# Summing attention weights on TensorE in place of VectorE, and moving small routing steps to GpSimd, in a kernel of two attentions and two expert layers

## The chip, the cores and the metric

The kernel runs on one core of a Trainium2 chip. The metric is the time of one execution on the device in microseconds (us), as the median of several runs. A core has five engines that run their own instruction streams in order and wait for one another by semaphores: TensorE (PE in the profile; its weight loads are listed as PEld), VectorE (DVE), ScalarE (ACT), GpSimd (POOL) and SyncE (SP), which issues most transfers. GpSimd issues the transfers that gather or scatter rows by a list of indices. All values here are 32-bit floats, save for some small bfloat16 tiles that are named below.

## The reference

Two layers, each an attention over a context and a feed-forward layer of eight experts, of which each row uses two. `x` is 4 x 512 x 256, the context 4 x 1601 x 256. The change lies in the second layer.

```python
x = x + _L0_xattn_ref(ctx_1024, _layernorm(x, axis=-1), ...)
x = x + _L0_ffn_ref(_layernorm(x, axis=-1), ...)
x = x + _L1_xattn_ref(ctx_1024, _layernorm(x, axis=-1), L1_xattn_Wq, L1_xattn_Wk, L1_xattn_Wv, 1, 0, 1)
x = x + _L1_ffn_ref(_layernorm(x, axis=-1), L1_ffn_W1, ...)
...
# _L1_xattn_ref: 8 heads of 32
attn = jnp.einsum('bhnd,bhmd->bhnm', q, k) * scale
attn = jax.nn.softmax(attn, axis=-1)
x = jnp.einsum('bhnm,bhmd->bhnd', attn, v)
...
# _L1_ffn_ref: the two largest logits of a row weigh its experts
logits = xf @ Wr + br
topv, _ = lax.top_k(logits, TOPK)
masked = jnp.where(logits >= topv[:, TOPK - 1:TOPK], logits, -jnp.inf)
weights = jax.nn.softmax(masked, axis=-1)
```

## The kernel before

The kernel runs in four stages: the first attention (up to about 1582 us of the span), the first expert layer (to 1885), the second attention (to 2430) and the second expert layer. The change touches the third, with one small piece at the end of the second.

**Units and passes.** The second attention is cut into 16 units: 4 batches, 2 groups of 4 heads, 2 halves of 256 queries. The 1601 keys are 13 tiles of 128 (the last has 65), taken in pairs, so a unit has 7 key pairs, 0 to 6; pair 6 is a single tile. `PER_UNIT` is 7. One loop (L1763) makes a pass for each pair of each unit. A pass does, in this order:

- `weights` (L1530): for the pair of this pass, PE writes four PSUM banks, one for each head. First it adds the negated row maxima (L1538, from the bfloat16 tile `below`), then the scores (L1548, keys by queries). ScalarE takes the exponentials into two tiles `pT` of 128 x 1024 (L1562); for pair 0 these tiles are named `sum`.
- `weigh` (L1573, matmul L1581): PE multiplies the weights of the pair of the pass before (`held`) with the values, into the left half of the PSUM tile `ps_o`.
- `add_weights` (L1568): if the held pair is in `ADDED`, VectorE adds its two tiles onto the `sum` tiles of the unit (L1571).
- `maxima` (L1264): PE computes a part of the scores of the next unit the other way round, queries by keys (L1281), into four more banks, and VectorE reduces each bank to row maxima (L1292). There are seven such parts a unit, the last of them short. They run ahead of the unit that uses them: those of unit u from pass 4 of unit u-2 to pass 3 of unit u-1, where the short one falls.
- `total` (L1590, matmul L1600): the sums of weights that the softmax divides by. PE multiplies weight tiles with ones, into the right half of `ps_o`. It does so for a held pair that is neither 0 nor in `ADDED`, and, when pair 6 is held, for the `sum` tiles too.
- `closing` (L1609), when pair 6 was held: the tile is copied out, turned back by PE two passes later (L1619, L1620), divided by the sums on VectorE (L1628, L1630) and added to `x` on GpSimd (L1637).
- a list of side work, `at[step]`.

So with `ADDED = (1, 3, 5)` VectorE adds in passes 2, 4 and 6 of a unit, and PE sums in passes 3 and 5 (pairs 2 and 4) and in pass 0 of the next unit (pair 6 and the `sum` tiles).

**PSUM.** Seven banks, handed out in turn, serve the weights, the maxima and all side work. A pass takes eight without side work, so the fourth bank of a pass's weights is the one that the first bank of the maxima before it held.

**Maxima to row.** `negated` (L1299) of unit u is put at the end of pass 4 of unit u-1: VectorE reduces the parts to `most` (L1303), then splits it into three bfloat16 pieces in the tile `shift`: three casts (L1311) and two subtractions (L1313), each on 128 x 8. `to_row` (L1315), at the end of pass 5, turns `shift` by a matmul (L1317), and ScalarE writes `below` from it (L1319), which L1538 of the next unit reads. `negated` of unit 0 runs in the stage before.

**Side work.** `project(b)` computes keys and values of batches 2 and 3 (L1166, L1182). `queries(b)` normalises `x` of the next batch (statistics on VectorE, the rows `xn` on GpSimd, L181), turns it (L194) and projects it (L1241). `collect` and `add_collected` gather rows of the first expert layer and add them to `x`, both on GpSimd (L359, L360, L379, L380). `route2(b)` routes batch b for the second expert layer, in some 28 parts spread over passes by the tuples `routed` and `last_routed`: normalised rows `pay` on GpSimd (L455, L463), logits, the two choices `hot`, the weights `wb`, a count of the rows that each expert has so far (`cnt`, `earlier`, `taken2`), from which PE computes places (L543, L546), and 16 scatters by GpSimd (L591). `by` in it is GpSimd for batches 0 to 2; for batch 3, which runs in the last stage, it is VectorE.

**Order.** The whole loop stands inside `in_order(*computing)` (L1753): PE, VectorE, ScalarE and GpSimd each execute in the order in which the program was written. An instruction that waits holds up all that is behind it on its engine.

```python
of = [(s, pTs)] if s and s not in ADDED else []
if s == PER_UNIT - 1:
    of.append((0, sums.pop(u)))
...
for u in range(1, n_units):
    put(PER_UNIT * (u - 1) + 4, lambda u=u: negated(u))
    put(PER_UNIT * (u - 1) + 5, lambda u=u: to_row(u))
```

Of the kernel before, what the change touches and what calls it, by code (L numbers as in the profile page):

```python
# [12 lines left out]
ALU = mybir.AluOpType  # L13
# [5 lines left out]
B, S, D = 4, 512, 256  # L19
# [28 lines left out]
FEW = (1, 5)  # L48
NOWHERE = 65536.0
PER_UNIT = -(-NM // 2)  # L50
ADDED = (1, 3, 5)

# [28 lines left out]
def xattn_ffn_twice(ctx: ExitStack, tc: tile.TileContext, a: dict, out: bass.AP):  # L83
    nc = tc.nc
# [315 lines left out]
    taken2 = const.tile([P, E], F32, name="taken2")  # L400
    nc.vector.memset(taken2, 0.0)
    taken_a = const.tile([P, E], F32, name="taken_a")
# [4 lines left out]
    extra = const.tile([P, NX, E], F32, name="extra")  # L407
# [29 lines left out]
    def route2(b, two, psum, tag, first=0, n=NT):  # L437

        by = nc.vector if b == B - 1 else nc.gpsimd
# [13 lines left out]
        pay = two.tile([P, n, PAY], F32, tag="pay", name="pay")  # L453
# [31 lines left out]
        def wide(name):  # L485
            return two.tile([P, n, E], F32, tag=name, name=name)
# [4 lines left out]
        def spread(t):  # L491
            return t.unsqueeze(2).to_broadcast([P, n, E])


        lg, wb, keep, rest = wide("lg"), wide("wb"), wide("keep"), wide("rest")
# [11 lines left out]
        nc.vector.tensor_reduce(tot, wb, AX.X, ALU.add)  # L507
        nc.vector.reciprocal(tot, tot)
        nc.vector.tensor_tensor(wb, wb, spread(tot), ALU.mult)
        nc.vector.tensor_copy(pay[:, :, D + 1 :], wb)  # L510
        yield


# [1 line left out]
        hot, chosen = [], []  # L515
# [10 lines left out]
                yield  # L526
        mine_b = slice(b * NT + first, b * NT + first + n)
        nc.vector.tensor_reduce(over[:, mine_b], rest, AX.X, ALU.add)
        nc.vector.tensor_tensor(extra[:, mine_b, :], rest, wb, ALU.mult)
        yield  # L530


        cnt, earlier = wide("cnt2"), wide("earlier2")
        nc.vector.tensor_tensor(cnt, hot[0], hot[1], ALU.add)
        for t in range(n):
            nc.vector.tensor_copy(earlier[:, t, :], taken2)
            nc.vector.tensor_tensor(taken2, taken2, cnt[:, t, :], ALU.add)
        if b == B - 2:
            nc.vector.tensor_copy(taken_a, taken2)
        yield  # L540
        ps = psum.tile([P, n, E], F32, tag=tag, name="ps_c2")
        flat = "p t e -> p (t e)"
# [61 lines left out]
        for t0 in range(0, n, 2):  # L604
            ps = psum.tile([P, 2, D], F32, tag=tag, name="ps_b2")
            for k in range(2):
                t = t0 + k
# [62 lines left out]
    with ExitStack() as st:  # L670
# [379 lines left out]
        for n in range(n_steps + 4):  # L1050
            b, h, t = n // (H0 * NT), n // NT % H0, n % NT
# [203 lines left out]
    rest = M // 512 * 512  # L1255
# [43 lines left out]
    def negated(u):  # L1299

        most = turns.tile([P, HG, 2], F32, tag="most", name="most")
        left = turns.tile([P, HG, 2], F32, tag="left", name="left")
        nc.vector.tensor_reduce(  # L1303
            most, tops[u].rearrange("q t i n -> q i t n"), AX.X, ALU.max, negate=True
        )
        tops.pop(u)
        part = shift[u % 2].rearrange("q (i c) -> q i c", i=HG)
        for k in range(PARTS):
            to = part[:, :, 2 * k : 2 * k + 2]
            of = left if k else most  # L1310
            nc.vector.tensor_copy(to, of)  # L1311
            if k + 1 < PARTS:
                nc.vector.tensor_tensor(left, of, to, ALU.subtract)  # L1313

    def to_row(u):  # L1315
        ps = banks["m"].tile([P, P], F32, tag="m", name="ps_r")
# [12 lines left out]
    with ExitStack() as st:  # L1329
# [117 lines left out]
        def keys_next():  # L1447
            *kv, steps = keys_values(ps_s, "s", 1)
            kvs.append(kv)
            steps[6:6] = [lambda: add_collected(0, got0)]  # L1450
            steps = iter(steps)
            asking = queries(0, qTs)

            for few, asks in ((4, 0), (5, 0), (3, 1), (0, 1), (2, 1), (0, 1), (1, 1), (1, 1), (0, 1)):
                for _ in range(few):
                    next(steps)()
                for _ in range(asks):
                    next(asking)
                yield
            assert next(steps, None) is None  # L1460

            firsts = [(0, g) for g in range(len(pieces))] + [(1, g) for g in range(3)]
            for k, (u, g) in enumerate(firsts):
                maxima(u, g)
                if (u, g) == (0, len(pieces) - 1):
                    negated(0)
                yield
                if k == 0:
                    next(asking)
                    assert next(asking, None) is None  # L1470
                if (u, g) == (1, 0):
                    to_row(0)
                if k % 2 == 0:
                    yield
# [34 lines left out]
    with ExitStack() as st:  # L1509
# [58 lines left out]
        def add_weights(u, s, pTs):  # L1568
            if s in ADDED:
                for to, pT in zip(sums[u], pTs):  # L1570
                    nc.vector.tensor_tensor(to, to, pT, ALU.add)  # L1571
# [18 lines left out]
        def total(u, s, pTs, ps):  # L1590

            of = [(s, pTs)] if s and s not in ADDED else []
            if s == PER_UNIT - 1:
# [105 lines left out]
# [4 lines that stand above are left out]
# [25 lines left out]
        for b in range(B):  # L1728
            s0 = per_batch * b
            if b:  # L1730
                place(s0, route2(b - 1, one, side, "s"), routed if b + 1 < B else last_routed)
            if b + 1 < B:
                got, steps = collect(b + 1)
                first = s0 if b == 0 else s0 - 14
                for k, f in enumerate(steps):
                    put(first + (k // 2 if b == 0 else k), f)
                for t in range(NT):
                    put(
                        (first + 4 if b == 0 else first + 7) + t // 2,
                        lambda b=b, got=got, t=t: add_collected(b + 1, got, (t,), nc.gpsimd),  # L1740
                    )
                place(s0, queries(b + 1, qTs), asked[b + 1])
# [45 lines left out]
    with ExitStack() as st:  # L1788
# [246 lines left out]
        def routing():  # L2035
            yield from route2(B - 1, two, ps_t, "t")
            yield from table()

        rest = routing()
# [14 lines left out]
        for i in range(n):  # L2054
            w, xT, to, share = here
# [153 lines left out]
```

## Time and profile before

| what | us |
|---|---|
| median of 3 runs | 2731.01 |
| lowest and highest of them | 2725.08, 2732.44 |
| the profiled execution | 2725.71 |
| its span, first to last instruction | 2724.0 |
| second attention in it | 1884.8 to 2430.0 |

The profile is one execution, recorded by the hardware. In its views a row names the line of the kernel, the engine and the operation, the tile that is written and those that are read, and how often. "Idle before" is time in which the engine had nothing to run, with what ended it. Matmuls overlap, so durations of single matmuls are not to be added; from the start of one group to the start of the next is the time that counts. A product of 32-bit values shows as two matmul instructions. A product whose output has 32 rows or whose contraction is 32 long uses a quarter of the array, and four of them for the four heads run side by side.

| second attention: line | what | count |
|---|---|---|
| L1548 PE | scores for the weights | 1664 |
| L1581 PE | weights by values | 1664 |
| L1281 PE | scores for the maxima | 936 |
| L1600 PE | sums by ones | 896 |
| L1292 DVE | row maxima | 408 |
| L1571 DVE | adds onto `sum` | 96 |

The counts are of instructions, of all forms and input tiles of a line.

### The profile page before, as it was taken

The page shows a single profiled execution, that of the slowest core. Times are in us where ns is not written, and L with a number is a line of the kernel's source. Part 1 is how long each engine was busy: PE and PEld are TensorE (multiplying, and loading weights), DVE is VectorE, ACT ScalarE, POOL GpSimd, SP SyncE. Part 2 cuts the span into 40 slices and gives each one's busy share as a digit, 9 for nine tenths or more (in the row PEclk, how much of TensorE's full clock was granted, in tenths as well). Part 3 has the DMA queues.
Part 4 walks back from the last instruction along what each step waited for, and adds up shares of the span by engine and source line. Part 5 has one row for each costly group of instructions (what it writes and reads, how often), then busy time and mean ns, then how long its engine had stood idle before and what let it go on. Part 6 is the DMA issues. An engine that isn't in the chain of part 4 may idle for free. (4 is left out here: it accounts for less than half of the span.)

```text
span 2724.0 us, 38199 instructions
## 1 busy us (share of the span) xinstructions
PE 2644.8 (97%) x14620; PEld 1795.0 (66%) x14620; DVE 1363.8 (50%) x2461; ACT 919.9 (34%) x1577; POOL 352.2 (13%) x372
## 2 busy tenths in 40 slices
PE   6999999999999999999999999899999999999998
PEld 3666676676666666767666678776454454468887
DVE  6444547544466544455444441124777878753111
ACT  4322334332334332333233221122444444452221
POOL 0000000100000100000100001102432421222542
PEclk9999999999999999999999999999999999999999
DMA  5444434433443343343343455453433200025673
GB/s 178 111 115 116 99 94 111 107 90 94 104 112 88 103 99 92 90 99 91 101 104 96 122 175 174 162 168 107 126 115 106 73 19 8 19 87 190 190 230 81
DMA packets 191323, 302.89 MB, mean 111 GB/s; under 512 B 41783, under 2 KB 113272, under 8 KB 188440
## 3 DMA queue, kind: packets, MB, share of 16 engines
q1 hardware_dynamic: 152392, 218.33, 28.8%
q0 software_dynamic: 14160, 46.31, 5.8%
q10 hardware_dynamic: 24576, 35.68, 5.2%
q8 instruction: 118, 1.93, 0.3%
q14 instruction: 77, 0.63, 0.1%
HBM read 111.46 MB, written 51.07 MB: 60 GB/s over the span
## 5 line engine op out<-in xcount | busy, mean ns | idle before, releaser
L949 DVE TENSOR_REDUCE top<-ps_s 128x1 f32<-128x2113 f32 x128 | 301.8, 2358 | 584.9 <-PE ps_s L941 584.0
L978 PE MATMUL ps_o<-pT,v 128*128 128x256 f32 x2176 | 519.5, 380 | 0.0
L941 PE MATMUL ps_s<-kT,qT 128*128 128x512 f32 (+1 forms) x1280 | 489.2, 526 | 6.1 <-ACT attn L955 5.9
L978 PEld LDWEIGHTS ps_o<-pT,v 128*128 128x128 f32 x2176 | 408.1, 190 | 110.7 <-issue 65.4
L955 ACT ACTIVATE attn<-ps_s,top 128x2113 f32<-128x2113 f32 x128 | 259.2, 2025 | 477.4 <-DVE top L949 458.4
L941 PEld LDWEIGHTS ps_s<-kT,qT 128*128 128x128 f32 x1280 | 241.7, 190 | 252.4 <-issue 236.0
L970 DVE STREAM_TRANSPOSE pT<-swapped 128x2176 f32<-128x2176 f32 x128 | 312.4, 2441 | 31.4 <-DMA swapped<-attn 22.5
L1292 DVE TENSOR_REDUCE tops<-ps_s 128x1 f32<-128x512 f32 (+2 forms) x428 | 251.5, 650 | 126.3 <-PE ps_s L1281 119.0
L887 PE MATMUL ps_k<-kvin,wkv 128*128 128x512 f32 (+2 forms) x640 | 259.3, 528 | 2.9 <-DVE kvin L807 2.4
L924 PE MATMUL ps_v<-wkv,kvin 128*128 128x256 f32 x1088 | 255.3, 381 | 2.2 <-ACT v L931 1.6
L1562 ACT ACTIVATE pT<-ps_w 128x512 f32<-128x512 f32 (+1 forms) x384 | 184.8, 567 | 140.4 <-PE ps_w L1548 138.4
L924 PEld LDWEIGHTS ps_v<-wkv,kvin 128*128 128x128 f32 x1088 | 204.7, 190 | 38.6 <-issue 6.0
L903 ACT ACTIVATE kT<-ps_k,bqk 128x512 f32<-128x512 f32 (+1 forms) x192 | 101.2, 556 | 260.4 <-PE ps_k L887 125.9
L887 PEld LDWEIGHTS ps_k<-kvin,wkv 128*128 128x128 f32 x640 | 115.7, 191 | 74.8 <-issue 63.3
L931 ACT COPY v<-ps_v 128x512 f32<-128x512 f32 x144 | 80.3, 562 | 212.9 <-PE ps_v L924 131.2
L1281 PE MATMUL ps_s<-kv,qT 32*128 32x512 f32 (+1 forms) x1024 | 129.1, 557 | 2.6 <-DVE got L1630 2.5
L1548 PE MATMUL ps_w<-qT,kv 32*128 32x256 f32 (+1 forms) x1664 | 120.4, 387 | 0.0
L1571 DVE TENSOR_TENSOR sum<-sum,pT 128x1024 f32<-128x1024 f32 x96 | 114.9, 1239 | 6.3 <-ACT pT L1562 6.3
L654 PE MATMUL ps_h<-sxT,w 128*128 128x256 f32 (+1 forms) x512 | 109.6, 371 | 4.0 <-DVE sxT L644 2.5
L1345 PE MATMUL ps_y<-w,hT 128*128 128x256 f32 x480 | 108.7, 382 | 0.0
L741 POOL TENSOR_TENSOR x<-x,bo 128x256 f32<-128x256 f32 x16 | 11.7, 762 | 742.2 <-DVE lat L181 544.9
L654 PEld LDWEIGHTS ps_h<-sxT,w 128*128 128x128 f32 x512 | 92.7, 192 | 21.5 <-issue 4.2
(317 smaller groups left out, 2766.9 us busy)
## 6 DMA issues: line engine op xcount, KB each, us to landing
swapped<-attn SPq DMA_DIRECT2D x1536, 68.0 KB
swapped<-attn ACTq DMA_DIRECT2D x512, 68.0 KB
w<-in_w_dram SPq DMA_DIRECT2D x32, 1024.0 KB
rows_b<-empty SPq DMA_DIRECT2D x36, 530.0 KB
w_e<-in_wall_dram SPq DMA_DIRECT2D x5, 2052.0 KB
cw<-in_ctxT_dram SPq DMA_DIRECT2D x4, 1601.0 KB
ctx_b<-in_ctx_dram SPq DMA_DIRECT2D x3, 1536.0 KB
slot_x<-scrap SPq DMA_DIRECT2D x8, 512.0 KB
```

The lines of the kernel that those rows point to most:

```text
L654: nc.tensor.matmul(ps[:, f, :], lhsT=w1[:, c, (f0 + f) * P : (f0 + f + 1) * P], rhs=sxT[:, c, :], start=c == 0, stop=c == DC - 1,)
L887: nc.tensor.matmul(ps[:, :n], lhsT=wkv[:, c, hs], rhs=kvin[:, c, : n // 32, k, :] if k < 4 else flat_kvin[c][:, left : left + P], start=c ...
L924: nc.tensor.matmul(ps[:, k, :], lhsT=flat_kvin[c][:, j * P : (j + 1) * P], rhs=wkv[:, c, cols], start=c == 0, stop=c == DC - 1,)
L941: nc.tensor.matmul(flat[:, j0 : j0 + n], lhsT=qT[:, t * P : (t + 1) * P], rhs=kT[:, j0 : j0 + n], start=True, stop=True,)
L949: nc.vector.tensor_reduce(top, flat[:, :L], AX.X, ALU.max, negate=True)
L955: nc.scalar.activation(attn[:, :L], flat[:, :L], AF.Exp, bias=top, accum_out=total)
L970: nc.vector.transpose(pT[:, :, k * P : (k + 1) * P].rearrange("p c (a i) -> p a c i", a=4), swapped.rearrange("p a (c i) -> p a c i", i=32),)
L978: nc.tensor.matmul(ps, lhsT=v[:, j - parts[part][0], (h % 2) * DH0 : (h % 2 + 1) * DH0], rhs=pT[:, j, :], start=j == 0, stop=j == NB - 1,)
L1281: nc.tensor.matmul(pss[i][:, at : at + n], lhsT=qTs[b][rows, o, q0 : q0 + P], rhs=kvs[b][0][o][rows, j0 : j0 + n], start=True, stop=True,)
L1292: nc.vector.tensor_reduce(tops[u][:, t : t + at // n, some, j0 // 512], of, AX.X, ALU.max,)
L1548: nc.tensor.matmul(pss[i][:r, k * QH : (k + 1) * QH], lhsT=kvs[b][0][o][rows, j * P : j * P + r], rhs=qTs[b][rows, o, f * QH : (f + 1) * Q ...
L1562: nc.scalar.activation(pT[:r, i, :n], pss[2 * h + i][:r, :n], AF.Exp)
```

## The change

`ADDED` becomes `(3,)`: VectorE adds only pair 3, in pass 4. Pairs 1 and 5 take the road of pairs 2 and 4: in passes 2 and 6 `total` multiplies their tiles with ones on PE. In `route2` a copy of the weights into `pay`, the product `extra` and the whole carried count go by `by`, which is GpSimd for batches 0 to 2. In `negated` the casts and subtractions go to GpSimd; the reduction to `most` stays on VectorE.

```diff
-ADDED = (1, 3, 5)
+ADDED = (3,)
...
-        nc.vector.tensor_copy(pay[:, :, D + 1 :], wb)
+        by.tensor_copy(pay[:, :, D + 1 :], wb)
...
-        nc.vector.tensor_tensor(extra[:, mine_b, :], rest, wb, ALU.mult)
+        by.tensor_tensor(extra[:, mine_b, :], rest, wb, ALU.mult)
...
         cnt, earlier = wide("cnt2"), wide("earlier2")
-        nc.vector.tensor_tensor(cnt, hot[0], hot[1], ALU.add)
+        by.tensor_tensor(cnt, hot[0], hot[1], ALU.add)
         for t in range(n):
-            nc.vector.tensor_copy(earlier[:, t, :], taken2)
-            nc.vector.tensor_tensor(taken2, taken2, cnt[:, t, :], ALU.add)
+            by.tensor_copy(earlier[:, t, :], taken2)
+            by.tensor_tensor(taken2, taken2, cnt[:, t, :], ALU.add)
         if b == B - 2:
-            nc.vector.tensor_copy(taken_a, taken2)
+            by.tensor_copy(taken_a, taken2)
...
         for k in range(PARTS):
             to = part[:, :, 2 * k : 2 * k + 2]
             of = left if k else most
-            nc.vector.tensor_copy(to, of)
+            nc.gpsimd.tensor_copy(to, of)
             if k + 1 < PARTS:
-                nc.vector.tensor_tensor(left, of, to, ALU.subtract)
+                nc.gpsimd.tensor_tensor(left, of, to, ALU.subtract)
```

## The prediction

> **What bounds the kernel now.** I read the page's busy table and slices first, then the stage of the change (the second attention, 1884.8 to 2430.0 us of the span) by windows, then PE's own timeline there, and last the lists of groups and waits.
>
> ```profile
> PE 2644.8 (97%) x14620; PEld 1795.0 (66%) x14620; DVE 1363.8 (50%) x2461; ACT 919.9 (34%) x1577; POOL 352.2 (13%) x372
> ...
> 1884.80:2430.00 545.20, 521.17 (x6050) 265.34 (x6053) 415.55 (x923) 262.00 (x553) 174.75 (x190) 0.98 0.22 67
> 1884.80:2160.00 275.20, 266.54 (x3059) 133.86 (x3062) 215.81 (x472) 134.70 (x286) 102.02 (x118) 1.00 0.34 102
> 2160.00:2310.00 150.00, 142.89 (x1652) 72.41 (x1648) 115.50 (x261) 70.82 (x148) 38.09 (x38) 0.99 0.10 36
> 2310.00:2402.00 92.00, 84.51 (x940) 43.26 (x940) 70.44 (x168) 38.41 (x82) 20.50 (x21) 0.89 0.05 15
> ```
>
> The columns of the windows are length, then busy time of PE, PEld, DVE, ACT and POOL, granted clock, DMA share, GB/s. PE is busy 521 of 545 us and DVE 416. So PE sets the pace, DVE has 130 us to spare, and VectorE work that is taken away is worth only the time that PE waits for it. The reader should also see the last row: 0.89 of the clock.
>
> PE's timeline gives those waits. The loop makes seven passes a unit; pass s runs L1538 and L1548 for key pair s, and L1581, the maxima L1281 and the sums L1600 for the pair before. Passes 6 and 0 of one unit:
>
> ```profile
> 2266.90 0.53 PE L1538 MATMUL ps_w<-below,ones_b 6*65 6x256 bf16 x4
> 2267.17 0.69 PE L1548 MATMUL ps_w<-qT,kv 32*65 32x256 f32 x8
> 2267.80 1.07 PE L1581 MATMUL ps_o<-pT,kv 128*32 128x256 f32 x16
> 2268.80 1.14 PE L1281 MATMUL ps_s<-kv,qT 32*128 32x512 f32 x8
> 2269.76 0.39 PE L1538 MATMUL ps_w<-below,ones_b 6*128 6x512 bf16 x3
> 2271.23 0.37 PE L1538 MATMUL ps_w<-below,ones_b 6*128 6x512 bf16 x1 [1.08 <-DVE tops L1292]
> ...
> 2274.56 1.05 PE L1600 MATMUL ps_o<-sum,ones 128*32 128x256 f32 x16
> ```
>
> ```profile
> 2268.23 2.35 DVE L1571 TENSOR_TENSOR sum<-sum,pT 128x1024 f32<-128x1024 f32 x2
> 2270.49 2.48 DVE L1292 TENSOR_REDUCE tops<-ps_s 128x1 f32<-128x512 f32 x4
> ```
>
> The fourth L1538 takes the bank of the first maxima; that reduction stands on DVE behind the two adds of key pair 5. Maxima started on PE at 2268.80, their reduction at 2270.49, PE went on at 2271.23. A start-to-start length shows the whole loss: L1538 takes 0.23 us where nothing waits and 1.48 here, and L1548 behind it 1.16 in place of 0.96.
>
> **The change, part by part.** *Sums on PE.* Pairs 1 and 5 leave VectorE in 16 units: 2 x 2 x 16 = 64 of the 96 adds, 64 x 1.24 = 79 us of DVE, nothing on the path by themselves. PE gains 2 pairs x 2 tiles x 4 heads = 16 products a unit, each two instructions in the trace, 512 in all. Sixteen L1600 take 1.00 us start to start in the passes that have them now (3, 5), so 32 x 1.00 = 32.0 us more PE time, all on the path; ends 0.95 and 1.05 a pass, 30.4 and 33.6.
>
> ```profile
> L1571 DVE TENSOR_TENSOR sum<-sum,pT 128x1024 f32<-128x1024 f32 x96 | 114.9, 1239 | 6.3 <-ACT pT L1562 6.3
> ...
> L1600 PE MATMUL ps_o<-pT,ones 128*32 128x256 f32 (+1 forms) x640 | 46.3, 400 | 0.0
> ```
>
> *Waits that go.* Adds of pairs 1 and 5 sit in passes 2 and 6, so the waits behind them are at the starts of passes 3 and 0. I took the length of each such pass from the first L1538 to the next pass's, less its side work, against the shortest of its kind: 3.80 us for pass 3 (units 5 and 9), 4.43 for pass 0 (unit 9). Half-clock stretches of L1581 and L1600 are left out here. Pass 3, units 0 to 14: 1.5, 1.5, 0.7, 1.5, 0.7, 0, 1.5, 2.2, 0.5, 0, 1.6, 1.3, 1.5, 2.6, 3.9, together 21.0. Pass 0, units 1 to 14: 0.6, 0.2, 0.6, 0.2, 0.1, 1.4, 0.5, 0.2, 0.2, 0.2, 1.5, 1.6, 0.7, 1.4, together 9.4. Maxima held up inside pass 6 of three units: 3 x 0.4 = 1.2. In all 31.6 us. Why all of it should go: the passes that follow passes 3 and 5, which have L1600 and no adds, start with 0.2 us of wait in nearly all units, since L1600 covers the first reduction (0.68). Lower end: passes 2 and 5 start in the bare units 11 to 14 with 0.9 us lost, behind a pass without L1600; if that much stayed in 9 places, 8 us less, 23.6. I take 31.6, as the new passes 2 and 6 look like 3 and 5.
>
> *xn.* Four L194 wait for GpSimd's normalised rows in three passes: 2.05, 2.47 and 3.12 us in place of 0.55, 6.0 lost. Two of the three normalisations follow pass-6 adds, the third runs beside them (6.59 us against 4.84). Their reductions could start only 0.6 us sooner, as the maxima end then; with the longer PE pass I take 3.0; ends 0 and 6.
>
> *Clock.* (1 - 0.89) x 92 + (1 - 0.99) x 150 = 11.6 us are lost to a half clock. The slow matmuls follow the longest waits above (units 8, 12, 13, 14), three of which shrink. I take 6; ends 0 and 11.
>
> [...] The row stands nearer to waits than to chance, so I keep 6.
>
> *Shift pieces.* Three casts and two subtractions a unit go from DVE (0.17 each, 0.205 from one to the next, 1.0 us in all) to GpSimd. The nearest GpSimd row is L463 (128x1), 0.27 mean; L380 (128x256) is 0.77 with 0.08 before its successor. For 8 elements I take 0.25 + 0.08, five times 1.65, and 0.3 for two handoffs: 2.0 us. What waits is L1317 on PE, with the whole loop behind it. From the end of `most` (L1303) to L1317 there are 3.4 us in the mean of the loop's fifteen units, 2.4 at least. So it costs 0; by L380's price the chain is 5 x 0.85 + 0.3 = 4.6 and L1317 late by some 1.2 us x 15 = 18. GpSimd's queue ahead of it: at unit 1 the eight gathers end at 1901, before `most` (1906.75); at units 6 and 10 the `pay` rows (L455) end at 2078.2 and 2226.2, `most` is at 2078.9 and 2226.9, and the adds taken from pass 2 bring more room. Behind it, the collected rows of batches 1, 2 and 3 now start 7 to 11 us later, and by my count end at 1925, 2000 and 2148 us; VectorE's statistics read the last two tiles at some 1929, 2004 and 2150. Nothing waits, narrowly in the last case.
>
> ```profile
> L380 POOL TENSOR_TENSOR x<-x,g 128x256 f32<-128x256 f32 x24 | 18.5, 773 | 2.0
> ...
> L463 POOL TENSOR_SCALAR pay<-lane 128x1 f32<-128x1 f32 x12 | 3.2, 270 | 0.3
> ...
> L1311 DVE CAST shift<-left 128x8 bf16<-128x8 f32 x30 | 5.7, 190 | 1.0
> ```
>
> [...]
>
> *Carried counts.* Eleven operations a batch for three batches, twelve in the last (L510, L529, L534 to L539): 34 x 0.2 = 7 us off DVE. On GpSimd the chain behind the second choice is about ten operations, 3.3 us (7.7 by L380); what waits is L543 on PE two passes on, some 8 us. Cost 0; the wait in pass 3 of unit 14 (3.9, counted above) has this chain in it. The last batch keeps VectorE.
>
> **Sum.** 32.0 - 31.6 - 3.0 - 6.0 = -8.6 us. The profiled execution took 2725.71 (span 2724.0 and 1.7 around it), 5.3 under the median of the runs; -8.6 gives 2717 from the one and 2722 from the other. I say 2720.
>
> **Rivals.** *Even trade* (0.24): the clock windows and the xn waits stay, 32.0 - 31.6 = 0, so 2726 to 2731. For it: two numbers of one size against each other. Against: the slow clock stands where the waits stand. *Late shift pieces* (0.12): GpSimd's chain at L380's price, 4.6 us and 1.2 late in each of 15 units: -8.6 + 18 = +9, 2735 to 2740. It decides from 0.57 us of lateness a unit, a chain of some 4.0 us or 0.74 an operation. Against: L463 at 0.27. *Everything goes* (0.08): all of xn and clock, 32.0 - 31.6 - 6 - 11 = -17, near 2709. That the sums are not moved can be left aside: which engine sums a pair hangs on one tuple that both helpers read, and the loop's order is fixed.
>
> **How the numbers follow.** Forecast 0.56 (2712 to 2728). A measurement of this kernel can tell about 0.3%, 8 us: faster is under 2722.8. Faster: 0.42 of the forecast, 0.02 of the even trade, 0.08: 0.52. Same: 0.14 + 0.21 + 0.01 = 0.36. Slower: 0.01 + 0.11 = 0.12. The range goes from the rival of everything, 3 us below it, to 5 over the median, where the late pieces begin: 2706 to 2736.
>
> **What would show it.** L1571 32 times; L1600 some 510 more, 1.0 us per sixteen; pass 3 at 3.8 and pass 0 at 4.4 us in nearly all units; waits of L1538 for L1292 down from 14.9 us to under 7, left in passes 2 and 5; granted clock over 0.95 between 2310 and 2400. Wrong if L1317 waits for GpSimd's L1311, if L1538 still waits in passes 3 and 0, or if the sixteen sums cost more than 1.05.

## The result, and the profile after

The kernel after the change takes 2740.53 us (median of 6 runs, 2737.24 to 2744.34); the kernel before, beside it, 2727.68 us (2724.39 to 2732.44, 6 runs). The ratio is 1.0042 with a 95% interval of 1.0031 to 1.0053: slower by 13 us (0.4%), where the prediction has 9 us less.

The profiled execution took 2739.64 us, its span 2737.9. The busy line and the groups that answer to those shown of before:

```profile
PE 2672.6 (98%) x15132; PEld 1805.9 (66%) x15132; DVE 1270.3 (46%) x2283; ACT 918.4 (34%) x1577; POOL 359.9 (13%) x486
```

```profile
L1600 PE MATMUL ps_o<-pT,ones 128*32 128x256 f32 (+1 forms) x1152 | 83.0, 389 | 0.6
...
L1571 DVE TENSOR_TENSOR sum<-sum,pT 128x1024 f32<-128x1024 f32 x32 | 37.8, 1221 | 1.6 <-ACT pT L1562 1.6
...
L1311 POOL CAST shift<-left 128x8 bf16<-128x8 f32 x32 | 6.1, 191 | 2.0
```

The change is there as described: 32 adds on VectorE in place of 96, 512 more L1600 on PE, the casts on GpSimd at 0.19 us each, which is VectorE's mean before. Outside the second attention the two spans have 2178.3 us before and 2174.8 after. The loss lies inside: from the first L1538 to the end of the last L1600 it is 545.7 us before and 563.1 after. The windows of the stage (columns as before: length, busy PE, PEld, DVE, ACT, POOL, granted clock, DMA share, GB/s), cut where those of before are cut as far as the shifted stage allows:

```profile
1881.70:2444.90 563.20, 551.01 (x6567) 276.98 (x6567) 322.71 (x750) 261.94 (x553) 184.18 (x302) 0.98 0.20 66
1881.70:2160.00 278.30, 276.04 (x3305) 137.45 (x3305) 167.25 (x388) 134.44 (x285) 103.00 (x169) 1.00 0.32 101
2160.00:2310.00 150.00, 147.30 (x1668) 73.34 (x1670) 86.00 (x195) 67.08 (x141) 39.17 (x66) 0.95 0.10 34
2310.00:2416.00 106.00, 98.91 (x1245) 49.78 (x1237) 64.39 (x161) 46.58 (x100) 34.60 (x60) 0.98 0.06 21
...
2401.00:2419.00 18.00, 15.50 (x153) 7.34 (x153) 3.53 (x22) 7.79 (x18) 8.88 (x13) 0.79 0.09 32
```

PE is now busy for 551 of 563 us, against 521 of 545 before. The waits that the prediction counted on are largely gone, as PE's list of waits shows (waits in total, times, longest):

```profile
PE ps_w L1538 <- DVE tops L1292: 5.3, 12, 1.5
PE ps_w L1548 <- issue: 2.3, 4, 1.0
PE ps_s L1281 <- DVE got L1630: 1.1, 1, 1.1
PE ps_w L1538 <- issue: 0.8, 1, 0.8
PE tp L194 <- POOL xn L181: 0.6, 1, 0.6
```

L1538 waited 14.9 us for L1292 before and 5.3 now, L194 4.4 us for `xn` and 0.6 now. What is new is "issue": PE stands for nothing that the profile shows. PE's timeline has the place, passes 5 and 6 of unit 14 and pass 0 of unit 15:

```profile
2402.72 1.07 PE L1581 MATMUL ps_o<-pT,kv 128*32 128x256 f32 x16
2403.60 1.05 PE L1600 MATMUL ps_o<-pT,ones 128*32 128x256 f32 x16
2404.58 0.23 PE L1317 MATMUL ps_r<-ident_b,shift 128*128 128x128 bf16 x1
2404.74 0.30 PE L1538 MATMUL ps_w<-below,ones_b 6*65 6x256 bf16 x4
2404.88 0.60 PE L1548 MATMUL ps_w<-qT,kv 32*65 32x256 f32 x8
2405.41 1.49 PE L1581 MATMUL ps_o<-pT,kv 128*32 128x256 f32 x16
2407.00 2.91 PE L1600 MATMUL ps_o<-pT,ones 128*32 128x256 f32 x16
2410.67 0.42 PE L1538 MATMUL ps_w<-below,ones_b 6*128 6x512 bf16 x4 [0.76 <-issue]
2412.10 2.65 PE L1548 MATMUL ps_w<-qT,kv 32*128 32x256 f32 x9 [1.00 <-issue]
```

Sixteen L1600 take 1.05 us at 2403.60 and 2.91 us at 2407.00; from the first of these to the next pass's L1538 it is 3.67 us in place of 0.98. And GpSimd's timeline has, from 2403.41 on, the scatters of the routing, one every 1.3 to 1.6 us:

```profile
2403.41 1.10 POOL L591 DMA_INDIRECT rows_a<-pay,place_a  x1 [0.55 <-DVE place L561]
2404.82 0.98 POOL L591 DMA_INDIRECT rows_b<-pay,place_b  x1 [0.30 <-DVE out_of L568]
2406.37 0.97 POOL L591 DMA_INDIRECT rows_a<-pay,place_a  x1 [0.57 <-issue]
2407.64 0.98 POOL L591 DMA_INDIRECT rows_b<-pay,place_b  x1 [0.30 <-issue]
```

After this stretch the granted clock falls for a while, to 0.50 from 2412 to 2425 us and 0.79 in the mean of the last row of the windows: L1548 at 2412.10 takes 2.65 us for nine matmuls, of which sixteen take 1.03 elsewhere.

### The profile page after: what moved, and what is told of

Read it like the earlier page. It is cut to its first block, busy times and chain, and to the rows that moved or that the text cites. A ratio compares the mean times of both kernels' runs of the same rounds, so it can differ in the third digit from the quotient of the medians.

```text
span 2737.9 us, 39139 instructions
## 1 busy us (share of the span) xinstructions
PE 2672.6 (98%) x15132; PEld 1805.9 (66%) x15132; DVE 1270.3 (46%) x2283; ACT 918.4 (34%) x1577; POOL 359.9 (13%) x486
## 5 line engine op out<-in xcount | busy, mean ns | idle before, releaser
L1292 DVE TENSOR_REDUCE tops<-ps_s 128x1 f32<-128x512 f32 (+2 forms) x428 | 252.2, 649 | 225.4 <-PE ps_s L1281 210.4
L970 DVE STREAM_TRANSPOSE pT<-swapped 128x2176 f32<-128x2176 f32 x128 | 312.4, 2441 | 30.4 <-DMA swapped<-attn 21.6
L1548 PE MATMUL ps_w<-qT,kv 32*128 32x256 f32 (+1 forms) x1664 | 122.5, 389 | 2.4 <-issue 2.3
L741 POOL TENSOR_TENSOR x<-x,bo 128x256 f32<-128x256 f32 x16 | 11.7, 759 | 743.0 <-DVE lat L181 545.3
L1345 PEld LDWEIGHTS ps_y<-w,hT 128*128 128x128 f32 x480 | 90.7, 192 | 15.0 <-issue 2.4
```

The costliest lines, as they stand in the source:

```text
L970: nc.vector.transpose(pT[:, :, k * P : (k + 1) * P].rearrange("p c (a i) -> p a c i", a=4), swapped.rearrange("p a (c i) -> p a c i", i=32),)
L1292: nc.vector.tensor_reduce(tops[u][:, t : t + at // n, some, j0 // 512], of, AX.X, ALU.max,)
L1345: nc.tensor.matmul(ps[:, t, :], lhsT=hT[:, f, t * P : (t + 1) * P], rhs=w2[:, f, :], start=f == 0, stop=f == FC - 1,)
```

## The experiments

After the first measurement there were eighteen more runs, in seven sets; the kernels of a set shared a chip and the runs of the kernel before. The kernel before does not take the same time in all of them, and that turned out to matter:

| set | chip | before, median us | kernels of the set |
|---|---|---|---|
| first measurement | not told | 2727.68 | the change |
| 1 | 12 | 2719.18 | sums alone, moves alone, sums left out, pair 1 only |
| 2 | 3 | 2727.55 | change again, before again, sums with pieces, sums with counts |
| 3 | 8 | 2719.28 | the change, sums alone, no scatters, pair 1 only |
| 4 | 9 | 2718.21 | the change, no scatters |
| 5 | 4 | 2724.00 | no scatters |
| 6 | 8 | 2729.14 | the change, no scatters |
| 7 | 14 | 2724.62 | pair 1 only |

I call sets 1, 3 and 4 (2718 to 2719 us) the first kind, the others (2724 to 2729 us) the second. These are medians; single runs of the two kinds overlap (2717.9 is the lowest in set 2, 2724.7 the highest in set 3).

**Set 1: one part of the change at a time.** Four kernels: only the sums move to PE; only GpSimd's work moves; the change with pairs 1 and 5 in no sum; the change with pair 5 back on VectorE.

```diff
 sums alone (on the kernel before)
-ADDED = (1, 3, 5)
+ADDED = (3,)
 moves alone (on the change)
-ADDED = (3,)
+ADDED = (1, 3, 5)
 sums left out (on the change)
-            of = [(s, pTs)] if s and s not in ADDED else []
+            of = [(s, pTs)] if s in (2, 4, 6) else []
 pair 1 only (on the change)
-ADDED = (3,)
+ADDED = (3, 5)
```

> Only ADDED = (3,) is taken over; the casts, subtractions and counts stay on VectorE. Theory 1 (late instructions): the sums buy back about the 31 us of waits that the forecast named, and the rest of the loss lies in stretches where PE, packed with short products, stands for nothing that the profile shows (2203 and 2406 us in the changed kernel), each followed by half-clock windows. Then this kernel is as slow as the change, 2736 to 2744, with the same kind of stretches. Theory 2 (the moves to GpSimd cost the time): back near the kernel before, 2718 to 2730. Theory 3 (the sums simply cost more than 1.0 us per sixteen): as slow as the change, with L1600 longer everywhere and no such stretches.

> ADDED stays (1, 3, 5); casts, subtractions and counts go to GpSimd. Theories 1 and 3: nothing to lose, a little less wait for L1292 (a unit's 1.0 us of VectorE work sits in pass 4, behind which PE waits little), 2720 to 2729. Theory 2: 2735 or more, with PE waiting at L1317 or L543 for GpSimd.

> The changed kernel without the sums of pairs 1 and 5 at all: neither engine adds them, so the softmax divides by sums that lack these pairs. This is the change with its price on PE taken away. If the price is the 32 us of L1600 alone (theory 3 without more): 2740 - 32 = 2708. Theory 1: the late stretches go with the packed products, so some 10 to 15 us more, 2693 to 2700. If waits for VectorE come back in passes 3 and 0, because L1600 no longer covers the first reduction: about 0.9 us x 30 passes given back, 2715 to 2730.

> The changed kernel with pair 5 back on VectorE, ADDED = (3, 5). PE saves 16 us of L1600; the waits at pass 0 come back (9 us by the count of the profile before). Theory 1: the late stretches at 2203 and 2406 us lie where passes 6 and 0 stand packed one behind the other, so they go too, 6 to 12 us: 2720 to 2728. Theory 3: 2740 - 16 + 9 = 2733.

Measured: sums alone 2714.22 us, ratio 0.9979 [0.9969, 0.9989]; moves alone 2714.07, 0.9978 [0.9969, 0.9988]; sums left out 2699.90, 0.9920 [0.9902, 0.9938]; pair 1 only 2705.83, 0.9952 [0.9935, 0.9968]. Each part of the change makes the kernel faster here, so no part is slow by itself, and the late shift pieces fall as an explanation: L1317 waits for GpSimd only 1.6 us in four places in all, and there the profile names L359 and L380 of the gathered rows, not the pieces L1311.

**Set 2: the parts together.** The change unaltered, the kernel before once more with a profile, and the sums with one of the two moves each.

```diff
 sums with pieces (on the change): counts back on VectorE
-        by.tensor_tensor(cnt, hot[0], hot[1], ALU.add)
+        nc.vector.tensor_tensor(cnt, hot[0], hot[1], ALU.add)
...
 sums with counts (on the change): pieces back on VectorE
-            nc.gpsimd.tensor_copy(to, of)
+            nc.vector.tensor_copy(to, of)
...
```

> The changed kernel itself, unaltered, beside the parts. Either part alone was 0.998 of the kernel before, the two together 1.004 in the result. Theory A (the two parts hurt each other: GpSimd's small steps beside denser products make PE stand without an instruction and drop its clock): 1.003 to 1.006 again, with stretches like those at 2203 and 2406 us. Theory B (nothing in the program joins them: the late stretches belong to the place of the first measurement and strike this kernel there): about the sum of the parts or a little better, 0.994 to 0.998, without such stretches.

> The kernel before, for a profile on this chip. Both theories: its time is that of the runs of the kernel before beside it; its waits in passes 3 and 0 as in the first profile (21 and 9 us). Tells whether the stages outside the second attention differ between the chips.

> ADDED = (3,) and the shift pieces on GpSimd; the carried counts, the copy into pay and extra back on VectorE. Theory A with the pieces at fault (L1317 waits for GpSimd, sixteen times): slower than before, 1.002 or more. Theory A with the counts at fault, or theory B: 0.994 to 0.998.

> ADDED = (3,) and copy, extra and counts on GpSimd; the shift pieces back on VectorE. Theory A with the counts at fault: 1.002 or more. Otherwise 0.994 to 0.998.

Measured: the change 2745.43 us, 1.0067 [1.0044, 1.0090]; before again 2726.19 (one run); sums with pieces 2744.52, 1.0069 [1.0044, 1.0094]; sums with counts 2741.29, 1.0058 [1.0038, 1.0078]. All three with the added sums are slower by the same. Whether that is so because the sums stand beside a move, or because this is another chip than in set 1, this set can't tell: it lacks the sums alone.

**Set 3: change and sums alone on one chip, and the scatters taken away.** The third kernel leaves the scatters of batches 0 to 2 out.

```diff
-                        nc.gpsimd.indirect_dma_start(
+                        if b == B - 1:
+                            nc.gpsimd.indirect_dma_start(
...
```

> The change unaltered, beside the three kernels below on one chip, so that chip and edit can be told apart. Every theory here: between 0.996 and 1.008 of the kernel before, as on the two chips so far; the ratio itself is the measure for the other three. If the cost belongs to some chips only, this chip shows it here by late TensorE instructions near the scatters at about 2200 and 2410 us and by half-clock windows after them, and the kernel before on this chip is then near 2727 us; on a chip that gives the kernel before about 2719 us they should be missing and the ratio be near 0.998.

> Only the sums: VectorE adds the pair of key tiles 3 alone, nothing moves to GpSimd. Theory 'sums': the late instructions come from the denser products beside the scatters, and which chip it is decides whether they come; then this kernel stands with the change within 0.3% on the same chip (about 1.004 to 1.007 where the change shows them, 0.998 where not). Theory 'moves': the sums are harmless and it takes the pieces or the counts on GpSimd to make them late; then 0.998 here again, about 15 to 20 us under the change, with the two late stretches missing from the profile.

> The change with the scatters of the first three batches (96 indirect transfers that GpSimd issues in the second attention) left out, so that the rows which they write keep what they were cleared with. Theory 'scatters': TensorE's instructions come late because the scatters run beside densely packed small products; without them no late stretches, no half-clock windows after them, the stage of the second attention 530 to 536 us in place of 560, and the time 0.990 to 0.996 of the kernel before. Theory 'density': the products alone outrun the supply of instructions; then the late stretches stay where few maxima run (passes 6 and 0), and the time is within 5 us of the change.

> The change with pair 5 in neither sum (VectorE adds only pair 3, TensorE sums 0, 1, 2, 4 and 6), as in the run of this name before, which gave 0.995 there: the total leaves out pair 5's weights. It has 256 products less of sums (16 us at 1.00 us a pass) than the change. Theory 'density in pass 6': the late stretches lie where pair 5's sums were put into pass 6, beside the scatters, and leaving these sums out takes the loss away too: 25 to 35 us under the change on this chip. Theory 'only the products': 14 to 18 us under the change, with the late stretches still in the profile.

The last expectation misdescribes its kernel: VectorE adds pair 5 there (`ADDED = (3, 5)`), and nothing is left out. And the scatters of three batches are 48, 16 a batch, not 96: the profile lists 56 scatter instructions (L591) with them and 8 without.

Measured: the change 2711.32 us, 0.9966 [0.9954, 0.9978]; sums alone 2712.95, 0.9973 [0.9965, 0.9982]; no scatters 2709.43, 0.9961 [0.9947, 0.9975]; pair 1 only 2707.98, 0.9958 [0.9944, 0.9972]. The unaltered change, slower twice, is now faster by 8 us, which is what had been forecast. It stands with the sums alone within 0.1%, so the moves do no harm in a set of the first kind; in the second kind the sums alone were never run. The kernel without scatters tells nothing here, as the change has no late stretches either.

**Sets 4 to 6: the pair that settles it.** The change and the change without scatters, until both met a set of the second kind.

> The change unaltered, to see which kind of chip this is and to stand beside the kernel below. Where the kernel before takes about 2719 us: 2711 us (0.996 to 0.998), no late stretches. Where it takes about 2727 us: 2737 to 2747 us (1.003 to 1.008), with late TensorE instructions and half-clock windows near 2200 and 2410 us.

> The change with the 96 scatters of the first three batches left out of the second attention (the rows that they write keep what they were cleared with). Only a chip on which the change is slower than the kernel before tells anything here. There, theory 'scatters': 2708 to 2716 us, no late stretches near 2200 and 2410 us, the stage of the second attention 528 to 536 us. Theory 'density': within 5 us of the change beside it, 2735 to 2747 us, with the same stretches. On the other kind of chip both give 2709 us, as in the run before.

> The change with the 96 scatters of the first three batches left out of the second attention, alone on one more chip. It tells something only where the kernel before takes about 2727 us rather than 2719 us, as on the two chips on which the change was slower than it. There, theory 'scatters': 2708 to 2716 us (0.993 to 0.996 of the kernel before), no late stretches near 2200 and 2410 us. Theory 'density': 2735 to 2747 us (1.003 to 1.008), with the stretches, though no scatter runs.

> The change unaltered, beside the kernel below. Where the kernel before takes about 2724 to 2728 us: 2735 to 2747 us (1.003 to 1.008), with late TensorE instructions near 2200 and 2410 us. Where it takes about 2719 us: 2711 us (0.996 to 0.998), without them.

> The change with the 96 scatters of the first three batches left out of the second attention, beside the change. Where the change is slower than the kernel before: theory 'scatters' 2708 to 2716 us, at least 20 us under the change and without late stretches; theory 'density' within 5 us of the change. Where the change is faster: both 2709 to 2712 us.

| set | the change | without scatters |
|---|---|---|
| 4 | 2711.02, 0.9972 [0.9960, 0.9985] | 2711.38, 0.9969 [0.9957, 0.9982] |
| 5 | not run | 2709.82, 0.9946 [0.9928, 0.9964] |
| 6 | 2737.87, 1.0043 [1.0027, 1.0058] | 2709.49, 0.9936 [0.9919, 0.9953] |

In set 6 the two kernels differ by 28.4 us; in sets 3 and 4, by 1.9 and -0.4. Without scatters the time is 2709 to 2711 us in all four sets; with them it is 2711 in one kind of set and 2738 in the other. The windows around the same place, for the change in set 6 (pass 6 of unit 14 to pass 1 of unit 15, three passes), for the change in set 3 and for the kernel without scatters in set 6 (pass 5 of unit 14 to pass 2 of unit 15, five passes):

```profile
2401.00:2421.00 20.00, 18.34 (x142) 8.58 (x138) 1.15 (x4) 6.67 (x16) 6.80 (x7) 0.74 0.08 28
```

```profile
2386.60:2403.30 16.70, 16.70 (x256) 10.14 (x259) 4.41 (x22) 11.60 (x26) 8.89 (x13) 1.00 0.20 67
```

```profile
2385.00:2401.50 16.50, 16.50 (x251) 9.98 (x247) 4.31 (x21) 11.46 (x26) 0.93 (x5) 1.00 0.10 34
```

The first count in brackets is PE's matmuls: 142 in 20 us, 256 in 16.7, 251 in 16.5. The reader should see that the second and third rows agree although GpSimd is busy 8.89 us in one and 0.93 in the other: in set 3 the scatters are there and cost PE nothing. In set 6 PE takes single matmuls about 0.7 us apart, as its timeline has it beside the same scatters:

```profile
2405.76 0.48 PE L1548 MATMUL ps_w<-qT,kv 32*128 32x256 f32 x1
2406.47 0.37 PE L1548 MATMUL ps_w<-qT,kv 32*128 32x256 f32 x1 [0.23 <-issue]
2407.18 2.21 PE L1548 MATMUL ps_w<-qT,kv 32*128 32x256 f32 x14 [0.34 <-issue]
2410.11 2.07 PE L1581 MATMUL ps_o<-pT,kv 65*32 65x256 f32 x7 [0.72 <-issue]
```

In set 3 the same instructions pass without a break:

```profile
2390.52 1.07 PE L1581 MATMUL ps_o<-pT,kv 128*32 128x256 f32 x16
2391.41 1.05 PE L1600 MATMUL ps_o<-pT,ones 128*32 128x256 f32 x16
2392.39 0.39 PE L1538 MATMUL ps_w<-below,ones_b 6*128 6x512 bf16 x4
2392.61 1.03 PE L1548 MATMUL ps_w<-qT,kv 32*128 32x256 f32 x16
2393.58 0.64 PE L1581 MATMUL ps_o<-pT,kv 65*32 65x256 f32 x8
```

The length of each of the 112 passes, from its first L1538 to the next pass's, makes the comparison exact. Between the change in set 6 and in set 3, passes that no scatter touches agree within 0.1 us, but for three that differ by 0.5, 0.8 and -1.6. Eleven passes beside the scatters hold 22.3 us, all of the difference of 22.1:

```
change, set 6 less set 3, us (passes that differ by over 0.2)
scatters of batch 0, 2169 to 2204 us: unit 8 pass 3 +0.3, pass 6 +0.7; unit 9 pass 0 +2.4
scatters of batch 1, 2303 to 2347 us: unit 12 pass 0 +1.8, pass 4 +0.5; unit 13 pass 0 +3.5, pass 1 +0.2
scatters of batch 2, 2400 to 2442 us: unit 14 pass 6 +1.8; unit 15 pass 0 +6.8, pass 1 +2.4, pass 5 +1.9
elsewhere: unit 0 pass 3 +0.5, pass 4 +0.8; unit 7 pass 4 -1.6
```

So the scatters make PE late, in the second kind of set: shown by leaving them out (28.4 us less in set 6). The lengths include the half clock behind each stretch. It is no separate cause here: the kernel without scatters has neither the stretches nor a half clock near them (one step of 3.4 us, at 2240).

The lateness reaches other engines, too. At the turn from unit 11 to 12 in set 6, beside the scatters of batch 1, VectorE begins the row maxima 3.4 us after the start of the products that they read, and PE has to wait for them:

```profile
2305.14 1.14 PE L1281 MATMUL ps_s<-kv,qT 32*128 32x512 f32 x8
2308.51 2.48 DVE L1292 TENSOR_REDUCE tops<-ps_s 128x1 f32<-128x512 f32 x4 [3.86 <-remote]
2309.26 0.37 PE L1538 MATMUL ps_w<-below,ones_b 6*128 6x512 bf16 x1 [1.55 <-DVE tops L1292]
```

In set 3 the same maxima begin 1.2 us after the start of their products, and PE doesn't wait:

```profile
2299.97 1.14 PE L1281 MATMUL ps_s<-kv,qT 32*128 32x512 f32 x8
2301.13 2.48 DVE L1292 TENSOR_REDUCE tops<-ps_s 128x1 f32<-128x512 f32 x4 [1.65 <-PE ps_s L1281]
```

"Remote" means that the signal which ended the wait came, but that the profile has no instruction ending near it. Here it is the signal that PE gives when a product is done. As the ends of matmuls are modelled, it can't be told whether the products were late or only their signals. That wait is most of the +1.8 in pass 0 of unit 12; behind the +1.9 in pass 5 of unit 15 is ScalarE, late in the same way by 1.9 us. In the second attention the ten traces of the first kind have no wait of this sort, and nine of the ten of the second kind have some (the exception is the first profile of the kernel before). The kernel without scatters in set 6 has one too, beside the gathers that open the stage (its lines stand one further down, so L1293 is L1292):

```profile
1895.22 0.90 DVE L1293 TENSOR_REDUCE tops<-ps_s 128x2 f32<-128x130 f32 x4 [3.28 <-remote]
```

Its pass 3 of unit 0 is 1.5 us longer there than in set 3. So here the same lateness goes with gathers, at the smaller price of 1.5 us.

**Set 7: half of the added sums, in the second kind.**

> The change with pair 5 back on VectorE (it adds pairs 3 and 5, TensorE sums 0, 1, 2, 4 and 6: nothing is left out, as in the two runs of this kind before), once more, for a chip on which the change is slower than the kernel before (that kernel at 2724 to 2729 us). There, if the late stretches need the products of pair 5's sums in pass 6 beside the scatters: 2706 to 2712 us, 0.992 to 0.996. If a part of them stays, as the kernel before has some there too: 2714 to 2722 us, 0.995 to 0.999. If it is the scatters beside any packed pass: 2725 us or more. On a chip of the other kind 2706 to 2708 us again.

Measured: 2736.84 us (2728.61 to 2745.31), 1.0051 [1.0033, 1.0069], where it gave 0.9952 and 0.9958 in the first kind. By pass lengths its profiled execution has 22.1 us more than that of set 3, of it 15.8 in passes 0 and 3.2 in passes 1, in units 8, 9, 12, 13 and 15. Its added products stand in passes 2, which have not grown at all. So it doesn't take pair 5's sums in pass 6 for the loss, nor are the added products the ones that come late; they are elsewhere, and the loss is as large.

## Why the prediction was wrong

With pass lengths one can read each term of the sum by itself. Moves alone (set 1) still has the three adds, the change of set 3 one; both are of the first kind, so the loss beside the scatters is not in the way. The first two rows are the profiled executions of the first measurement:

```
us in the second attention, passes of 16 units added up
pass                 0      1      2      3      4      5      6    sum
before, first       86.3   74.5   73.5   91.4   73.3   74.3   72.2  545.3
change, first       91.0   80.0   89.4   69.8   71.6   75.6   85.4  562.8
moves alone, set 1  87.5   76.2   72.9   90.1   72.2   74.3   65.5  538.8
change, set 3       75.8   74.5   89.4   68.3   72.7   74.3   81.0  536.1
change, set 6       90.4   77.1   89.4   69.2   72.4   76.2   83.6  558.2
no scatters, set 6  75.8   74.5   89.4   69.8   71.1   74.3   81.0  536.0
pair 1 only, set 3  87.6   76.0   89.4   68.0   71.1   74.3   65.2  531.6
```

*Sums on PE*, forecast 32.0: passes 2 and 6 grow by 16.5 and 15.5, together 32.0, 1.00 a pass in most units. Right, where nothing makes PE late.

*Waits that go*, forecast 21.0 for pass 3 and 9.4 for pass 0, with 1.2 inside pass 6: 21.8 and 11.7 are measured. Right in place, and so is the reason: in set 3 L1538 waits for L1292 2.5 us in all, against 14.3 with the moves alone. The size is near, but these lengths hold the half clock too, of which 8.5 us go (below); what is left for the waits is 25 to 33.5 us, by an estimate from these numbers (forecast 30.4).

```profile
PE ps_w L1538 <- DVE tops L1292: 14.3, 32, 1.6
```

```profile
PE ps_w L1538 <- DVE tops L1292: 2.5, 9, 0.4
```

*xn*, forecast 3.0: L194 waits 3.8 us less after. Right.

*Shift pieces* and *carried counts*, forecast 0: not late in any run. Moves alone is even 5.1 us faster than the kernel before (0.9978). I had no term for that. The kernel before has no profile in a set of the first kind, so where these 5 us come from stays open. The rival of late shift pieces is refuted; the chain of five took 1.3 us (0.27 from one to the next) where I had put 1.65, and 0.3 for handoffs.

*Clock*, forecast -6. The reason, that "the slow matmuls follow the longest waits above", agrees with the clock's records. In the kernel before, PE is at half clock from 2353 to 2360 and from 2391 to 2401 us (granted 0.51 and 0.50; sixteen L1581 take 1.94 us there and 1.07 elsewhere), right behind waits of L1538 for L1292 of 1.0 and 1.5 us that end at 2351.6 and 2388.6; the third batch of scatters begins only at 2402.5. In the first kind of set, 23.9 us of the stage are at half clock with the moves alone and 6.8 with the change. Half of the difference is lost time that goes, 8.5 us by an estimate from these numbers. In the first measurement it is 23.9 us before and 27.3 after, so the term came out at 1.7 more instead of 6 less; in set 6 it is 13.7 with the change, some 5 us less lost than in the two profiles of the kernel before (23.9 in each), and the change was slower there all the same. The half clock behind the waits went in the first measurement too: the sign that I wrote down, over 0.95 between 2310 and 2400, was met. But new half clock came behind the late stretches, from 2207 to 2214 and from 2412 to 2425 (granted 0.53 and 0.50), beside the first and the third batch of scatters.

*The step that failed* is the path. "32 x 1.00 us, all on the path" and 9.4 us off passes 0 hold all else in a pass to be constant: nothing is put for what GpSimd's transfers do to the other engines, and I never laid their times next to the passes. From the first row of the table to the second, passes 2 and 6 grow by 29.1 (forecast 32.0 - 1.2) and passes 3 lose 21.6 (21.0): as forecast. But passes 0 grow by 4.7 where they were to lose 9.4, and passes 1 grow by 5.5 where nothing was put. In units 9, 13 and 15, beside the scatters, passes 0 and 1 grow by 16.7 together, and pass 6 of unit 14 grows by 4.3 where the sums need 1.0 (there sixteen of them took 2.91 us). Against set 3 the change of the first measurement has 26.7 us more in the passes, nearly all of it in such places, and the kernel before has lost less there: its median differs by 5 to 11 us between the kinds. None of my rivals was this one; the slower one that I had named costs nothing.

So the forecast of -8.6 us is met in sets 3 and 4 (-8.0 and -7.2) and missed by 17 to 27 us where the change ran in the second kind (13, 18 and 9 us over the kernel before). That it is met is in part luck: from the moves alone to the change of set 3 all of my terms together give -2.7 us (538.8 to 536.1), and the moves, which I had put at 0, give 5.1. The sums alone give 5.0 and 6.3 (sets 1 and 3).

What stays open. The difference between the kinds is not shown: the kernels are the same, and chip 8 gave both (2711 us in set 3, 2738 in set 6), so it isn't the chip's number alone. It is also open what about the scatters holds the engines up (their issue by GpSimd, their descriptors, or the rows that they write), since leaving them out takes all of it away; and why the kernel before loses so much less by them than all kernels with added sums, though the late passes are not those that got more products. Each kernel with added sums that ran with scatters in the second kind has at least one of the moves as well, so there it isn't shown that the sums alone are enough; and the kernel before was not run without the scatters. Beside the third batch of scatters the profile's queue q8, named "instruction" (122 packets, 2.00 MB, so 16 KB each), has one packet 15.8 us after the one before in set 6 and 7.5 us after it in set 3; in the first measurement it is 17.0 us there. Whether the longer gap holds PE up or follows from its lateness isn't shown, so this doesn't decide it. The late signals to VectorE and ScalarE don't decide it either. And the traces of the second kind lack some records of PE's signals (14 of 1094 in the stage in set 6, 1 in set 3), so a part of the recorder in this isn't ruled out.

No version here is shown to be faster in both kinds. Pair 1 only is the best in the first (0.9952 and 0.9958): pair 5's sums cost 15.8 us in pass 6 and win back 11.8 in pass 0 and 1.5 in pass 1. Moves alone and sums alone have not been run in the second.

## What to carry to other kernels

Where a trade of two terms of equal size decides (32.0 against 31.6 here), the outcome hangs on what neither term holds; lay the times of everything that runs beside the stage, indirect transfers above all, next to the slow passes before giving a half clock or a long pass a cause. Compare pass lengths and not busy times: between two executions of one kernel they agreed within 0.1 us in nearly all passes, so that a handful of others shows where the disturbance is. And measure a change of less than 1% in more than one set, with the kernel before in each: the verdict of one chip, 1.0067 or 0.9966, was each time firm within its interval and said the opposite of the other.

## What the runs showed of the hardware

Beside GpSimd's indirect scatters (0.97 us each in the median; in the first measurement one every 1.3 to 1.6 us from 2403 us on), PE started single L1548 about 0.7 us apart in set 6, of which sixteen take 1.03 us in set 3, though by the profile it waits for none of the scatters; VectorE and ScalarE, too, began on PE's products some 2 us later there than in set 3. It came in some sets and not in others with the same program, and cost the kernels with added sums 22 to 33 us in 560 (least in sets 6 and 7, most in set 2).

The half clock came in steps of 3.4 us, up to 13.7 us at a stretch in the first measurement (from 2412 to 2425 us), and the longest wait that PE's timeline has from 2395 to 2425 us is 1.0 us. What sets it off isn't shown: in the kernel before, two stretches stand behind waits of 1.0 and 1.5 us; in the first measurement, two stand beside the scatters.
